# Layers 1 and 2 of a gated graph network: h turned by DMA instead of TensorE, and the adjacency loaded twice

## The chip, the cores and the metric

The kernel runs on one core of a Trainium2 chip. The metric is the device time of one execution in microseconds (us). The engines of the core work side by side, each through its own queue in order: PE (TensorE, matmuls, with PEld for its weight loads), DVE (VectorE), ACT (ScalarE), POOL (GpSimd) and SP (SyncE, which here issues nearly all DMA transfers).

## The reference

There are 64 graphs of N = 256 nodes with D = 256 features each, and a 0/1 adjacency matrix for each. First come three layers of a gated graph network, then a residual and a normalization, then one graph attention layer with another residual and normalization:

```
A = (adj != 0)
h = x
for i in range(3):
    m    = h @ weight[i]
    aggr = A^T @ m                      # per graph: 'bst,bsd->btd'
    h    = gru_cell(aggr, h)            # r, z, n gates of 256 columns each
x = layernorm(x + h)
Wh = x @ W ; s1 = Wh @ a1 ; s2 = Wh @ a2
e  = leaky_relu(s1[:, None] + s2[None, :]) ; e = where(adj > 0, e, -9e15)
out = layernorm(x + softmax(e) @ Wh)
```

The kernel aggregates h before it multiplies by the weight (the weight is folded into the input weights of the gates once, at the start), so each layer needs A^T h and then matmuls with fixed weights.

## The kernel before

**Tiling.** The 64 graphs are taken in 32 pairs (G = 2). The state h of a pair is kept turned, as `hT`: features on the 128 partitions (two halves, d = 0 and 1), the 512 nodes of the two graphs along the free dimension. It is updated in place by each layer. The adjacency of a pair is loaded once by `load_adj` (line 170) into a buffer of the pool `io` that has one copy only (tag "adj"); `ones` (line 318) makes the fp32r matrix A of it, and `masking` (line 327) makes a uint8 mask that is kept, in four buffers, until the pair's attention, some three turns later.

**Split precision.** Matmuls run in fp32r. Operands are cut into an upper part and a rest: `hi` and `lo` for the aggregation, and pieces H, L and D of h and of the aggregate for the gates (`upper`, `lower`, `cross`, lines 128 to 136).

**A layer.** `front(p, i, t, pace)` prepares layer i of pair p. The aggregation wants h with the nodes on the partitions, so `turn` (line 337) transposes `hT` on PE: `from_T` (line 308) issues four 128x128 transposes for each half d into one PSUM bank "pt". ACT casts the bank to `hi` (line 349) and DVE subtracts for `lo` (line 133 through `lower`). For layer 0, x itself already has the nodes on the partitions, and no transpose is needed. `aggregate` (line 375) issues 8 matmuls a half into a bank "pa"; `a_upper` and `a_rest` cut the result. `gates` (line 400) then runs 8 products of 6 or 12 matmuls of 128x512, each into a bank "pga" and a bank "pgb"; ACT evacuates pga, DVE adds pgb, ACT applies sigmoid or tanh, POOL multiplies and blends, and DVE writes the new half of `hT` (line 451).

**PSUM.** There are eight banks of 512 fp32 columns, handed out in rotation by `bank` (line 106) to every user on PE.

**Attention.** `attention(p, t)` (line 490) reads x back, adds h in the turned layout (`vT`), and turns that sum by transfers: `turn` (line 501) issues two DMA transposes, which move 16-bit elements, so that the fp32 words come out as interleaved 16-bit rows in the buffer "wh"; `second` (line 511) gathers low and high halves with four transfers into the buffer "sc"; `join` (line 519) puts them together through `put_together` (line 278), ACT writing the high halves and DVE the low ones. Then follow a normalization, the projection (`project`, L541), scores, the mask (`masked`, L573), softmax, and the combination (L601). The tile in "wh" serves first as the buffer of the transposes and then for the projected features, and the tile in "sc" first for the halves and then for the scores.

**x by transfers.** For pairs from 5 on (`FROM` = 5), x_turned (line 284) and x_joined (line 302) produce `hT` of layer 0 in the same way: a DMA transpose of x into the buffer "x" of `io`, a gather into the buffer "adj" of `io`, and a join on ACT and DVE.

**The order of the work.** It is written out by hand. A clock counts ticks, which advance inside `gates` (12 ticks a block). A step registered with `at(t, step)` or `after(dt, step)` is issued when the clock reaches its tick, and each engine's queue has the instructions in that order. The blocks (pair, layer) are interleaved: a turn of 36 ticks holds layer 0 of pair q, layer 1 of pair q-1 and layer 2 of pair q-2, while the attention of pair q-3 runs beside them. The offsets within a layer's preparation are the tuples `CLOSE`, `LOOSE` and `FIRST` (lines 621 to 623): the first tuple gives the ticks of turn, hi, lo, aggregate, a_upper and a_rest, and the second those of the pieces H, L and D of h.

Of the kernel before, what the change touches and what calls it, by code (L numbers as in the profile page):

```python
# [9 lines left out]
F32 = mybir.dt.float32  # L10
# [9 lines left out]
P = 128  # L20
# [7 lines left out]
def kernel(  # L28
# [230 lines left out]

    pairs = {}  # L260

    def room(kind, shape, p):


        name = f"{kind}_{p}"
        if p < NP - 2:
            return late.tile(shape, F32, tag=kind, name=name, bufs=2 if kind == "v" else 1)
        tag = {"v": "hH", "vT": "hD", "wh": "aH", "sc": "aD"}[kind]
        return work.tile(shape, F32, tag=tag, name=name)
# [5 lines left out]
            nc.tensor.transpose(pt[:, k * P:(k + 1) * P], src[:, k // C, k % C, d * P:(d + 1) * P], ident)  # L275
        after(1, lambda: evacuate(dst[:, d, :], pt))

    def put_together(dst, hi, lo):

        dst = dst.bitcast(U16).rearrange("p (n h) -> p n h", h=2)  # L280
        nc.scalar.copy(dst[:, :, 1], hi)
        nc.vector.tensor_copy(dst[:, :, 0], lo)

    def x_turned(p):

# [38 lines left out]
    def take_x(p):  # L324
        pairs[p].x = loaded.pop(p)

    def masking(p):
        s = pairs[p]
        s.mask = work.tile([P, K, N], U8, tag="mask", name=f"mask_{p}", bufs=4)
        nc.vector.tensor_scalar(s.mask, s.adj.rearrange("p g c n -> p (g c) n"), 0.0, None, op0=ALU.is_le)  # L330

    def front(p, i, t, pace):

        nm = f"{p}_{i}"
        hi, lo, src = [None] * C, [None] * C, [None] * C

        def turn(d):
            s = pairs[p]
            if i == 0:
                if p < FROM:  # L340
                    to_T(s.x, s.hT, d)
            else:
                src[d] = from_T(s.hT, d).rearrange("p (k n) -> p k n", k=K)

        def split(d):
            if i == 0:
                src[d] = nodes(pairs[p].x, d)
            hi[d] = work.tile([P, K, P], F32R, tag=f"hi{d}", name=f"hi{d}_{nm}", bufs=1)
            nc.scalar.copy(hi[d], src[d])
# [24 lines left out]

        def aggregate(d):
            s = pairs[p]
            if d == 0:
                s.ag = pieces(work, [P, C, GN], nm, "a")
            pt = src[d] = bank("pa")
            for g in range(G):  # L380
                todo = [(h[d], c) for c in range(C) for h in (hi, lo)]
                for n, (h, c) in enumerate(todo):
                    nc.tensor.matmul(pt[:, g * N:(g + 1) * N], h[:, g * C + c, :], s.A[:, g, c, :],  # L383
                                     start=(n == 0), stop=(n == len(todo) - 1))

        def a_upper(d):
            upper(pairs[p].ag[0][:, d, :], src[d])

        def a_rest(d):
            H, Lo, Di = [t[:, d, :] for t in pairs[p].ag]  # L390
            lower(nc.vector, Lo, src[d], H)
            cross(Di, src[d], H)

        for d in range(C):
            for dt, step in zip(pace[0], (turn, split, rest, aggregate, a_upper, a_rest)):
                at(t + dt + d, lambda step=step, d=d: step(d))
        for dt, step in zip(pace[1], (h_upper, h_lower, h_cross)):
            at(t + dt, step)
# [91 lines left out]
    def attention(p, t):  # L490
# [10 lines left out]
        def turn(d):  # L501

            if d == 0:
                s.wh = room("wh", [P, G, C, D], p)
                s.first = s.wh.rearrange("p g c d -> p (g c d)").bitcast(U16).rearrange(
                    "p (k b d) -> p k b d", b=2, d=D)
            nc.sync.dma_start_transpose(
                s.first.rearrange("p k b d -> p (k b) d")[:, :, d * P:(d + 1) * P],
                s.vT[:, d, :].bitcast(U16))

        def second():
            s.sc = room("sc", [P, K, N], p)
            s.halves = s.sc.rearrange("p k n -> p (k n)").bitcast(U16).rearrange(
                "p (h k d) -> p h k d", h=2, k=K)
            for h in range(2):
                for b in range(2):
                    nc.sync.dma_start(s.halves[b * 64:b * 64 + 64, h], s.first[h::2, :, b])

        def join(g):
            if g == 0:  # L520
# [13 lines left out]

        def project(k):
            if k == 0:
                s.s1 = work.tile([P, K], F32, tag="s1", name=f"s1_{p}")
                s.s2 = s.sc[:, :, :P]
            pts[k] = bank("pwh")
            for d in range(C):  # L540
                nc.tensor.matmul(pts[k][:, :D + 2], s.vT[:, d, k * P:(k + 1) * P], gw[:, d, :],  # L541
                                 start=(d == 0), stop=(d == C - 1))

        def spread(k):
            rs = s.rs[:, k:k + 1]
            for dst, src in ((s.s1[:, k:k + 1], pts[k][:, D:D + 1]),
                             (s.s2[:, k, :], pts[k][:, D + 1:D + 2].to_broadcast([P, P])),
                             (s.wh[:, k // C, k % C, :], pts[k][:, :D])):
                if k < 2:
                    nc.scalar.activation(dst, src, AF.Copy, scale=rs)  # L550
                else:
                    nc.vector.tensor_scalar(dst, src, rs, None, op0=ALU.mult)
        for k in range(K):
            at(t + 35 + k, lambda k=k: project(k))
            at(t + 36 + k, lambda k=k: spread(k))

        def rows():
            pts[0] = bank("s2")
# [3 lines left out]
        def scores():  # L562
            for k in range(K):
                nc.scalar.activation(s.sc[:, k, :], pts[0][:, (k // C) * N:(k // C + 1) * N], AF.Prelu,
                                     bias=s.s1[:, k:k + 1], alpha=ALPHA)
        at(t + 40, rows)
        at(t + 41, scores)

        s.nm = work.tile([P, K], F32, tag="nm", name=f"nm_{p}")
        s.sm = work.tile([P, K], F32, tag="sm", name=f"sm_{p}")  # L570

        def masked():
            nc.vector.copy_predicated(flat(s.sc), flat(s.mask), neg.to_broadcast([P, K * N]))  # L573
        at(t + 42, masked)
        at(t + 43, lambda: nc.vector.tensor_reduce(s.nm, s.sc, AX.X, ALU.max, negate=True))

        def exps(k):
            nc.scalar.activation(s.sc[:, k, :], s.sc[:, k, :], AF.Exp, bias=s.nm[:, k:k + 1],
# [69 lines left out]
    nc.vector.tensor_add(b_sum, bi, bh)  # L648
    tick()
    ones(0)  # L650
    masking(0)
    load_adj(1)
    tick()
    for parts in PARTS:
# [16 lines left out]
    for n, (p, i) in enumerate(blocks):  # L671
        if n + 1 < len(blocks):
            np_, ni = blocks[n + 1]
            if ni == 0:
                if np_ < FROM:
                    after(1, lambda p=np_: begin(p))
                after(1, lambda p=np_: take_x(p))
                after(2, lambda p=np_: ones(p))
                nxt = np_ + 1
                if nxt < FROM:  # L680
                    after(7, lambda p=nxt: load_x(p))
                elif nxt < NP:
# [12 lines left out]
    while pending:  # L695
        clock[0] = pending[0][0]
        run_due()
# [29 lines left out]
```

## Time and profile before

The three runs took 2168.55 to 2170.91 us, with a median of 2169.64 us; the profiled execution took 2168.29 us, and its span in the trace is 2166.5 us.

| engine | busy, us | share | instructions |
|---|---|---|---|
| PE (matmul) | 2124.7 | 98% | 10508 |
| PEld | 1790.7 | 83% | 10508 |
| DVE | 1735.2 | 80% | 2885 |
| POOL | 1593.0 | 74% | 1114 |
| ACT | 1497.1 | 69% | 2734 |
| DMA queue q1 | | 27.1% of 16 engines | 234816 packets |

A group row of the profile gives line, engine, operation, output and input tile, shape and count, then the total busy time and the mean duration of one in ns, then the idle time of the engine just before these instructions and what ended it. The chain of waits is followed back from the last instruction; its shares tell what set the end. A turn of the steady state lasts 65.1 us (from 999.8 to 1064.95 us in the trace, at the first layer-0 product of two neighbouring turns).

### The profile page before, as it was taken

The numbers are of one execution on the slowest core, as the hardware profiler recorded it, in microseconds if no ns is written. First come the engines' busy times: TensorE is split into PE (matmuls) and PEld (weight loads), VectorE is DVE, ScalarE is ACT, GpSimd is POOL, SyncE is SP. The second block draws the span as 40 slices with busy tenths as digits, with TensorE's granted clock in tenths as the row PEclk, the third lists the DMA queues.
The fourth block names the chain that finished last, engine by engine and source line by source line (L and its number), as shares of the span: only waits on it lengthen the run. The fifth ranks groups of instructions, "written<-read, shape, count | busy, mean of one in ns | idle before, by whom it ended". The sixth has DMA issues, their size and how long they took to land.

```text
span 2166.5 us, 30928 instructions
## 1 busy us (share of the span) xinstructions
PE 2124.7 (98%) x10508; PEld 1790.7 (83%) x10508; DVE 1735.2 (80%) x2885; ACT 1497.1 (69%) x2734; POOL 1593.0 (74%) x1114
## 2 busy tenths in 40 slices
PE   8999999999999999999999999999999999999995
PEld 6788888888888888888888888888888888888873
DVE  5667878888778888778888788888788888788786
ACT  4566677677777677777677777677777677777664
POOL 6688677777777777777777777777777777787671
PEclk9999999999999999999999999999999999999997
DMA  3001322322322222322323323323323223321122
GB/s 117 30 30 49 79 69 69 78 74 64 88 66 71 76 72 67 88 64 74 74 70 72 88 61 76 71 69 76 88 59 78 69 69 78 86 61 49 39 54 64
DMA packets 236765, 150.39 MB, mean 69 GB/s; under 512 B 130304, under 2 KB 228352, under 8 KB 236608
## 3 DMA queue, kind: packets, MB, share of 16 engines
q1 hardware_dynamic: 234816, 146.58, 27.1%
q8 instruction: 84, 1.38, 0.3%
q10 hardware_dynamic: 1616, 1.57, 0.2%
q14 instruction: 73, 0.60, 0.1%
q0 software_dynamic: 176, 0.27, 0.1%
HBM read 52.96 MB, written 33.55 MB: 40 GB/s over the span
## 4 chain that ended last, share of the span: by engine, by line
PE 95%; DVE 2%; POOL 1%; ACT 1%; DMA 0%; issue 0%; POOLq 0%; ACTq 0%; SPq 0%; DVEq 0%
PE pga L412 48%; PE pgb L412 24%; PE pa L383 8%; PE po L601 5%; PE pwh L541 5%; PE pt L311 3%; PE pt L593 1%; PE s L560 1%; DMA rows_hH<-in_L_gnn_w_hh_dram 0%; PE pw L236 0%; POOL t L438 0%; POOL wc2L_wc L147 0%; POOL t L439 0%; DVE v L607 0%; DVE cut L133 0%
## 5 line engine op out<-in xcount | busy, mean ns | idle before, releaser
L438 POOL TENSOR_TENSOR t<-hT,n 128x512 f32<-128x512 f32 x192 | 273.0, 1422 | 392.0 <-ACT n L430 391.8
L412 PE MATMUL pga<-hH,whhH_whh 128*128 128x512 f32 x1152 | 375.7, 407 | 0.0
L412 PE MATMUL pga<-hL,whhL_whh 128*128 128x512 f32 x1152 | 357.6, 392 | 1.0 <-POOL hL L133 1.0
L412 PE MATMUL pgb<-hD,whhD_whh 128*128 128x512 f32 x1152 | 357.5, 391 | 1.0 <-DVE hD L136 1.0
L448 POOL TENSOR_TENSOR n<-n,t 128x512 f32<-128x512 f32 x192 | 274.9, 1432 | 77.8 <-DVE t L421 67.5
L417 ACT ACTIVATE r<-pga 128x512 f32<-128x512 f32 x192 | 114.4, 596 | 289.6 <-PE pga L412 163.4
L439 POOL TENSOR_TENSOR t<-t,z 128x512 f32<-128x512 f32 x192 | 303.4, 1580 | 15.0
L412 PEld LDWEIGHTS pga<-hL,whhL_whh 128*128 128x128 f32 x1152 | 216.3, 188 | 49.2 <-POOL hL L133 1.5
L444 POOL TENSOR_TENSOR n<-n,r 128x512 f32<-128x512 f32 x192 | 256.0, 1333 | 0.9 <-DVE n L421 0.9
L412 PEld LDWEIGHTS pgb<-hD,whhD_whh 128*128 128x128 f32 x1152 | 216.4, 188 | 48.6 <-DVE hD L136 1.4
L133 POOL TENSOR_TENSOR hL<-hT,hH 128x1024 fp32r<-128x1024 f32 x96 | 242.8, 2529 | 11.2 <-ACT hH L130 11.1
L412 PEld LDWEIGHTS pga<-hH,whhH_whh 128*128 128x128 f32 x1152 | 200.4, 189 | 26.6
L419 ACT ACTIVATE n<-pga,bh 128x512 f32<-128x512 f32 x192 | 132.1, 688 | 117.8 <-PE pga L412 112.5
L383 PE MATMUL pa<-A,hi 128*128 128x256 f32 x768 | 202.3, 297 | 0.2 <-DVE A L322 0.2
L421 DVE SCALAR_TENSOR_TENSOR r<-pgb,r 128x512 f32<-128x512 f32 x192 | 131.4, 685 | 82.1 <-ACT r L417 57.1
L383 PE MATMUL pa<-A,lo 128*128 128x256 f32 x768 | 192.2, 283 | 0.0
L136 DVE SCALAR_TENSOR_TENSOR hD<-hH,hT 128x1024 fp32r<-128x1024 f32 x96 | 190.5, 1985 | 0.0
L451 DVE TENSOR_TENSOR hT<-t,n 128x512 f32<-128x512 f32 x192 | 165.6, 863 | 4.3 <-POOL t L439 4.3
L421 DVE SCALAR_TENSOR_TENSOR n<-pgb,n 128x512 f32<-128x512 f32 x192 | 131.2, 683 | 44.4 <-ACT n L419 44.4
L421 DVE SCALAR_TENSOR_TENSOR t<-pgb,t 128x512 f32<-128x512 f32 x192 | 131.2, 683 | 39.4 <-ACT t L417 38.5
L417 ACT ACTIVATE t<-pga 128x512 f32<-128x512 f32 x192 | 114.6, 597 | 68.1 <-PE pga L412 68.1
L430 ACT ACTIVATE r<-r,b_sum 128x512 f32<-128x512 f32 x192 | 139.2, 725 | 23.1 <-DVE r L421 22.6
(138 smaller groups left out, 5365.2 us busy)
## 6 DMA issues: line engine op xcount, KB each, us to landing
x<-in_x_dram SPq DMA_DIRECT2D x32, 512.0 KB, 3.9
adj<-in_adj_dram SPq DMA_DIRECT2D x32, 512.0 KB, 3.9
xT<-hT SPq DMA_DIRECT2D x32, 512.0 KB, 4.1
vT<-xT SPq DMA_DIRECT2D x32, 512.0 KB, 3.6
sc<-wh SPq DMA_DIRECT2D x128, 128.0 KB, 3.4
out_dram<-v SPq DMA_DIRECT2D x32, 512.0 KB, 3.0
second<-first SPq DMA_DIRECT2D x108, 128.0 KB, 3.0
wh<-vT SPq DMA_TRANSPOSE x64, 3.2
```

What stands on the lines that cost most here:

```text
L133: eng.tensor_sub(dst, src, hi.bitcast(F32))
L136: nc.vector.scalar_tensor_tensor(dst, hi.bitcast(F32), 1.0 + U, src, op0=ALU.mult, op1=ALU.subtract)
L383: nc.tensor.matmul(pt[:, g * N:(g + 1) * N], h[:, g * C + c, :], s.A[:, g, c, :], start=(n == 0), stop=(n == len(todo) - 1))
L412: nc.tensor.matmul(pt, w[:, d, o * P:(o + 1) * P], m[:, d, :], start=n in (0, ends + 1), stop=n in (ends, len(todo) - 1))
L417: nc.scalar.activation(dst, a, AF.Copy, scale=1.0 + U)
L421: nc.vector.scalar_tensor_tensor(dst, b, -1.0 / U, dst, op0=ALU.mult, op1=ALU.add)
L430: nc.scalar.activation(dst, dst, func, bias=bias)
L438: nc.gpsimd.tensor_sub(t, h, n)
L439: nc.gpsimd.tensor_mul(t, t, z)
L444: after(2, lambda r=r, n=n: nc.gpsimd.tensor_mul(n, n, r))
L448: after(1, lambda n=n, t=t: nc.gpsimd.tensor_add(n, n, t))
L451: after(lags[2], lambda n=n, t=t, h=h: nc.vector.tensor_add(h, t, n))
```

## The change

For layers 1 and 2 of pairs 5 to 30 (layer 2 up to pair 29), `hT` is turned by transfers instead of on PE. The new `h_turned(p, i, e)` is registered after the gates of layer i: two DMA transposes and a gather of four transfers on SP, and for each half d a join (both 16-bit halves on ACT, into a tile "V" with one buffer), a cast to `hi` on ACT and a subtraction for `lo` on DVE. For the turning after layer 0 it borrows the buffers "wh" and "sc", and after layer 1 the buffers "x" and "adj" of `io`. `front` then skips its first three steps. The other pairs and layers keep the transposes on PE.

To make room, the buffers "wh" and "sc" are released by attention between its two uses of them; its projection comes two ticks later, and so do the scores, the masking and the maximum. The mask is no longer made with A and kept: the adjacency is loaded a second time (`adj_again`), and the mask is made from it just before its use, in one buffer instead of four. The steps of x and of the adjacency are moved by some ticks, and layer 2 from pair 5 on uses `CLOSE` in place of `LOOSE`.

```diff
-    def put_together(dst, hi, lo):
+    def put_together(dst, hi, lo, k=None):
...
-        dst = dst.bitcast(U16).rearrange("p (n h) -> p n h", h=2)
-        nc.scalar.copy(dst[:, :, 1], hi)
-        nc.vector.tensor_copy(dst[:, :, 0], lo)
+        dst = dst.bitcast(U16).rearrange("p (n h) -> p h n", h=2)
+        if k:
+            dst = dst.rearrange("p h (k n) -> p h k n", k=k)
+        nc.scalar.copy(dst[:, 1], hi)
+        if k:
+            nc.scalar.copy(dst[:, 0], lo)
+        else:
+            nc.vector.tensor_copy(dst[:, 0], lo)
...
+    def h_turned(p, i, e):
...
+        s = pairs[p]
+        pool, tags, dt = ((late, ("wh", "sc"), (16, 19, 22)), (io, ("x", "adj"), (12, 22, 25)))[i]
...
+        def first():
+            tmp["a"] = first_of(pool.tile([P, G, C, D], F32, tag=tags[0], name=f"first_h{p}_{i}"))
+            for d in range(C):
+                turn_half(tmp["a"], s.hT, d)
...
+        def second():
+            tmp["b"] = second_of(pool.tile([P, G, C, D], F32, tag=tags[1], name=f"second_h{p}_{i}"))
+            gather(tmp["b"], tmp["a"])
...
+        def join(d):
+            tmp[d] = work.tile([P, K, P], F32, tag="V", name=f"V{d}_{p}_{i}", bufs=1)
+            put_together(tmp[d].rearrange("p k n -> p (k n)"),
+                         *(tmp["b"][:, h, :, d * P:(d + 1) * P] for h in (1, 0)), k=K)
...
+        at(e + dt[0], first)
+        at(e + dt[1], second)
+        for d in range(C):
+            for n, step in enumerate((join, split, rest)):
+                at(e + dt[2] + 3 * d + n, lambda step=step, d=d: step(d))
+        s.by_dma = i + 1
...
-    def masking(p):
-        s = pairs[p]
-        s.mask = work.tile([P, K, N], U8, tag="mask", name=f"mask_{p}", bufs=4)
-        nc.vector.tensor_scalar(s.mask, s.adj.rearrange("p g c n -> p (g c) n"), 0.0, None, op0=ALU.is_le)
...
         for d in range(C):
-            for dt, step in zip(pace[0], (turn, split, rest, aggregate, a_upper, a_rest)):
+            for dt, step in list(zip(pace[0], (turn, split, rest, aggregate, a_upper, a_rest)))[3 * by_dma:]:
                 at(t + dt + d, lambda step=step, d=d: step(d))
...
         for k in range(K):
-            at(t + 35 + k, lambda k=k: project(k))
-            at(t + 36 + k, lambda k=k: spread(k))
+            at(t + 37 + k, lambda k=k: project(k))
+            at(t + 38 + k, lambda k=k: spread(k))
...
-        at(t + 40, rows)
-        at(t + 41, scores)
+        at(t + 42, rows)
+        at(t + 43, scores)
...
+        at(t + 38, adj_again)
+        at(t + 43, mask)
...
-        at(t + 42, masked)
-        at(t + 43, lambda: nc.vector.tensor_reduce(s.nm, s.sc, AX.X, ALU.max, negate=True))
+        at(t + 44, masked)
+        at(t + 45, lambda: nc.vector.tensor_reduce(s.nm, s.sc, AX.X, ALU.max, negate=True))
...
-                after(2, lambda p=np_: ones(p))
+                after(3, lambda p=np_: ones(p))
...
-                    after(22, lambda p=nxt, d=later: d.update(f=x_turned(p)))
-                    after(26, lambda d=later: d["f"]())
-                    after(30, lambda p=nxt: x_joined(p))
-                    after(31, lambda p=nxt: load_x(p))
-                early = 3 if np_ + 1 < FROM else 0
-                after(19 - early, lambda p=np_: masking(p))
-                after(20 - early if nxt < FROM else 32, lambda p=nxt: load_adj(p))
-            front(np_, ni, clock[0], CLOSE if n and np_ == blocks[n - 1][0] else LOOSE if ni else FIRST)
+                    after(25, lambda p=nxt, d=later: d.update(f=x_turned(p)))
+                    after(29, lambda d=later: d["f"]())
+                    after(32, lambda p=nxt: x_joined(p))
+                    after(32, lambda p=nxt: load_x(p))
+                after(5 if nxt < FROM else 34, lambda p=nxt: load_adj(p))
+            front(np_, ni, clock[0], 
+                  CLOSE if n and np_ == blocks[n - 1][0] or ni == 2 and np_ >= FROM else LOOSE if ni else FIRST)
...
         if i == L - 1:
             attention(p, clock[0])
+        elif FROM <= p and p + i + 1 < NP:
+            h_turned(p, i, clock[0])
```

More of the change, by code (lines that the diff above doesn't have):

```diff
@@ L260, with room @@
     pairs = {}
-    def room(kind, shape, p):
-        name = f"{kind}_{p}"
+    def room(kind, shape, p, name=None):
+        name = f"{name or kind}_{p}"
         if p < NP - 2:
@@ new lines, in first_of, with second_of, turn_half, gather @@
+    def first_of(t):
+        return t.rearrange("p g c d -> p (g c d)").bitcast(U16).rearrange("p (k b d) -> p k b d", b=2, d=D)
+    def second_of(t):
+        return t.rearrange("p g c d -> p (g c d)").bitcast(U16).rearrange("p (h k d) -> p h k d", h=2, k=K)
+    def turn_half(dst, src, d):
+        nc.sync.dma_start_transpose(dst.rearrange("p k b d -> p (k b) d")[:, :, d * P:(d + 1) * P],
+                                    src[:, d, :].bitcast(U16))
+    def gather(dst, src):
+        for h in range(2):
+            for b in range(2):
+                nc.sync.dma_start(dst[b * 64:b * 64 + 64, h], src[h::2, :, b])
@@ new lines, in h_turned, with split, rest @@
+    def h_turned(p, i, e):
+        s = pairs[p]
+        pool, tags, dt = ((late, ("wh", "sc"), (16, 19, 22)), (io, ("x", "adj"), (12, 22, 25)))[i]
+        tmp = {}
+        def first():
[9 more added lines that the diff above has]
+                         *(tmp["b"][:, h, :, d * P:(d + 1) * P] for h in (1, 0)), k=K)
+        def split(d):
+            s.hi[d] = work.tile([P, K, P], F32R, tag=f"hi{d}", name=f"hi{d}_{p}_{i + 1}", bufs=1)
+            nc.scalar.copy(s.hi[d], tmp[d])
+        def rest(d):
+            s.lo[d] = work.tile([P, K, P], F32R, tag=f"lo{d}", name=f"lo{d}_{p}_{i + 1}", bufs=1)
+            lower(nc.vector, s.lo[d], tmp[d], s.hi[d])
+        s.hi, s.lo = [None] * C, [None] * C
+        at(e + dt[0], first)
[4 more added lines that the diff above has]
+        s.by_dma = i + 1
@@ L325, in take_x @@
         pairs[p].x = loaded.pop(p)
-    def masking(p):
-        s = pairs[p]
-        s.mask = work.tile([P, K, N], U8, tag="mask", name=f"mask_{p}", bufs=4)
-        nc.vector.tensor_scalar(s.mask, s.adj.rearrange("p g c n -> p (g c) n"), 0.0, None, op0=ALU.is_le)
     def front(p, i, t, pace):
         nm = f"{p}_{i}"
+        by_dma = getattr(pairs.get(p), "by_dma", None) == i
         hi, lo, src = [None] * C, [None] * C, [None] * C
+        if by_dma:
+            hi, lo = pairs[p].hi, pairs[p].lo
         def turn(d):
@@ L503, in turn @@
             if d == 0:
[L504 to L509, printed above, removed]
-        def second():
[L512 to L517, printed above, removed]
+                s.first = first_of(room("wh", [P, G, C, D], p, "first"))
+            turn_half(s.first, s.vT, d)
+        def second():
+            s.halves = second_of(room("sc", [P, G, C, D], p, "second"))
+            gather(s.halves, s.first)
         def join(g):
@@ L536, in project @@
             if k == 0:
+                s.wh = room("wh", [P, G, C, D], p)
+                s.sc = room("sc", [P, K, N], p)
                 s.s1 = work.tile([P, K], F32, tag="s1", name=f"s1_{p}")
@@ L565, in scores, with adj_again, mask @@
                                      bias=s.s1[:, k:k + 1], alpha=ALPHA)
-        at(t + 40, rows)
-        at(t + 41, scores)
+        at(t + 42, rows)
+        at(t + 43, scores)
         s.nm = work.tile([P, K], F32, tag="nm", name=f"nm_{p}")
         s.sm = work.tile([P, K], F32, tag="sm", name=f"sm_{p}")
+        def adj_again():
+            load_adj(p)
+        def mask():
+            s.mask = work.tile([P, K, N], U8, tag="mask", name=f"mask_{p}", bufs=1)
+            nc.vector.tensor_scalar(s.mask, loaded_adj.pop(p).rearrange("p g c n -> p (g c) n"), 0.0, None,
+                                    op0=ALU.is_le)
+        at(t + 38, adj_again)
+        at(t + 43, mask)
         def masked():
             nc.vector.copy_predicated(flat(s.sc), flat(s.mask), neg.to_broadcast([P, K * N]))
-        at(t + 42, masked)
-        at(t + 43, lambda: nc.vector.tensor_reduce(s.nm, s.sc, AX.X, ALU.max, negate=True))
+        at(t + 44, masked)
+        at(t + 45, lambda: nc.vector.tensor_reduce(s.nm, s.sc, AX.X, ALU.max, negate=True))
         def exps(k):
@@ L650 @@
     ones(0)
-    masking(0)
     load_adj(1)
```

## The prediction

> **What bounds the kernel now.** I read the page's busy table first, then the chain that ended last, then the groups for the lines that the diff touches, then one turn of the steady state (1000 to 1065 us) engine by engine, and last the waits of SP's queue.
>
> ```profile
> PE 2124.7 (98%) x10508; PEld 1790.7 (83%) x10508; DVE 1735.2 (80%) x2885; ACT 1497.1 (69%) x2734; POOL 1593.0 (74%) x1114
> ...
> PE pga L412 48%; PE pgb L412 24%; PE pa L383 8%; PE po L601 5%; PE pwh L541 5%; PE pt L311 3%; PE pt L593 1%; PE s L560 1%; DMA rows_hH<-in_L_gnn_w_hh_dram 0%; PE pw L236 0%; POOL t L438 0%; POOL wc2L_wc L147 0%; POOL t L439 0%; DVE v L607 0%; DVE cut L133 0%
> ```
>
> ```profile
> 1000.00:1065.00 65.00, 65.00 (x326) 55.06 (x324) 53.70 (x90) 46.50 (x86) 49.33 (x35) 1.00 0.29 73
> ```
>
> In that window (columns: PE, PEld, DVE, ACT, POOL busy, clock, DMA share, GB/s) PE has no idle time in 65.00 us, while DVE has 11.3, ACT 18.5 and POOL 15.7. The chain is 95% PE, and the transposes that the change takes off PE (L311) are on it with 3%. So a PE instruction removed shortens the span, and one added elsewhere costs nothing until PE waits for it.
>
> ```profile
> L311 PE MATMUL pt<-ident,hT 128*128 128x128 f32 x512 | 77.1, 273 | 0.0
> L349 ACT CAST hi<-pt 128x512 fp32r<-128x512 f32 x128 | 74.6, 583 | 7.1 <-PE pt L311 7.1
> L133 DVE TENSOR_TENSOR lo<-pt,hi 128x512 fp32r<-128x512 f32 x128 | 87.6, 686 | 11.3 <-ACT hi L349 11.2
> L281 ACT COPY hT<-second 128x512 uint16<-128x512 uint16 x54 | 37.6, 768 | 0.0
> L451 DVE TENSOR_TENSOR hT<-t,n 128x512 f32<-128x512 f32 x192 | 165.6, 863 | 4.3 <-POOL t L439 4.3
> ```
>
> ```profile
> 1003.64 1.03 PE L541 MATMUL pwh<-gw,vT 128*128 128x258 f32 x4
> 1004.51 0.60 PE L311 MATMUL pt<-ident,hT 128*128 128x128 f32 x4
> 1004.86 0.72 PE L412 MATMUL pga<-hH,whhH_whh 128*128 128x512 f32 x2
> 1005.42 0.40 PE L412 MATMUL pga<-hL,whhL_whh 128*128 128x512 f32 x1
> ```
>
> The last fence is the timeline of PE (start, length). From the start of four transposes to the start of hL is 0.91 us, and two 128x512 matmuls alone take 2 x 0.227; so a group of four costs 0.455 us. Over the 69 groups of the trace that stand between L412 matmuls the median is the same 0.4545 us.
>
> ```profile
> SPq L616 <- ACT v L478: 563.0, 32, 19.6
> SPq L173 <- DVE hT L282: 331.5, 27, 12.5
> SPq L299 <- DVE mask L330: 128.9, 27, 5.5
> SPq L517 <- DMA wh<-vT: 60.4, 34, 3.1
> ```
>
> These are waits of SP's queue. It issues in order, and stands for long stretches behind a store or an adjacency load; nothing on PE waits for it now.
>
> **What the Trainium skill says.** "TensorE: Matmul & The Clock Gate", Part 4: PE-mode transpose, gives about 275 ns for one in a kernel; the trace has 273 ns as a duration, but only 0.455/4 = 0.114 us of PE's time, which is what counts. "DMA: Bandwidth & Descriptors", DMA Transpose (X-bar), allows 2-byte types only, which is why an fp32 tile goes as 16-bit halves and must be rejoined; the uint16 copies of L281 are that price. Its Rules for kernel authors say that a DMA reading what an earlier DMA wrote must wait for its completion: the 60.4 us of L517 above. "SBUF — State Buffer", Who interferes with whom: a DVE instruction with two SBUF inputs contends with a GpSimd one that reads SBUF; the trace agrees (L451 863 ns against 686 for the PSUM form of L133), and says that ACT waits for nobody.
>
> **The change part by part.** A turn is three blocks, 36 ticks, 65.1 us. Layer-1 turning through DMA is made for pairs 5 to 30, layer-2 for 5 to 29: 51 times.
>
> Removed from PE: 51 x 2 groups of four = 408 of 512 transposes, 102 x 0.455 = 46.4 us. Bounds: the busy column, 77.1/512 x 408 = 61.4 us, is the high end (it shares out overlap); I take the start-to-start value. Two PSUM banks less per turned layer are also taken.
>
> Added to ACT: 204 copies (hi and lo of each half-tile, both on ACT) x 0.768 = 156.7 us; 102 casts read SBUF instead of PSUM, 609 against 583 ns (the row of hi<-x), 2.7 us. That is 6.2 us a turn on 18.5 idle; ACT goes to about 1656 us, 78% of the new span. It matters only as lateness: where copies stand ahead of the evacuations of pga, banks come free later. In the trace I matched each bank's last reader with the matmul that takes the bank eight allocations later: typically 3 to 6 us lie between, with 1.2 and 0.3 us at 1028.3 and 1030.2. The 0.3 us is a bank of the removed transposes. Layer 2's joins come just there (ticks 13 to 17, about 1023 to 1031), behind the exponentials, where ACT has no gap from 1020.0 to 1029.2. PE comes there 0.9 to 1.8 us sooner, ACT is about 1 us later, and after re-counting the banks without the transposes' two, 1.5 us are left at the tightest place. Layer 1's joins (ticks 34 to 38, about 1061 to 1068) make ACT at most 2 us later against 4 to 5 us of margin; the spread of the attention moved two ticks back makes room. I count 0 to 1 us of PE wait a turn, taken as 2 us in all.
>
> DVE: 102 subtractions now have two SBUF inputs, 0.68 to 0.86 us, so 0 to 18 us, and POOL may lose as much as 102 x 0.68 = 69 us (its twins run 1.29 us alone and up to 2.16 beside such an instruction), 2.7 us a turn on 15.7 idle. The 32 masks stay 32, now made beside the scores. Hidden behind PE both.
>
> SP and DMA: added are 102 half transposes, 204 gathers, 32 adjacency loads. Issue: 1.32 us a transpose, 2.6 for four gathers, 0.4 a load: 10.9 us a turn. Occupancy from the packet records of the window: 1.26 us of all engines a half transpose, 2.9 four gathers, 1.8 a load, so 4 x 1.26 + 2 x 2.9 + 1.8 = 12.7 us on 19; the share goes from 0.29 to about 0.50. The adjacency buffer (one) gets four tenants a turn: the adjacency, its reload, layer 2's second half, the x second half. Past SP's queue I followed one turn in before's times. Mask done about 1014, gather 1016, landed 1019; join wants it at 1023: 4 us spare. The x transpose then lands at 1024; its gather waits for the second join on ACT, 1030, is issued until 1032.4 and landed about 1035; behind it stand load x, the attention's transposes (which wait for L601 until 1035.6 anyway) and load adj. x_joined wants it at about 1036. Attention's gather lands about 1047.5; layer 1's transposes follow, then the stash, then its gather 1053.5 to 1056, landed 1058 to 1059; ACT wants it at 1058.7. This is the tightest: 0 to 1 us of wait on ACT, inside the bank margin.
>
> The moves: projection and spread +2 ticks, scores to maximum +2 with the exponentials unmoved, x turning +3, ones +1, layer 2's aggregation +1 with hL and hD earlier: all order only, with PE's work unchanged. At the end, one group of four pwh matmuls goes behind the last gate product, and the mask for pair 31 loads only after a store waiting for ACT (2137.8 before) and a landing of 3.9 us, so about 2142.5 against its use at 2143.5: 0 to 2 us, taken as 1.
>
> Sum against the profiled span of 2166.5: -46.4 + 2 + 1 = -43.4, so 2123.1; the median of the runs is 3.1 above that span, which gives 2169.6 - 43.4 = 2126.
>
> **The rivals.** (A) The forecast: hidden, 2117 to 2136.
> (B) Half is given back: ACT late by the joins at both places, PE waiting about 0.9 us a turn for banks, 26 x 0.9 = 23, so 2149 (2136 to 2162). For: ACT has no gap at the table loads. Against: the large gaps (3.4 us at 1035.6) right after, and fewer banks taken.
> (C) No change: transposes filled time that PE would wait anyway, 2165 to 2174. Against: PE's idle before L311 is 0.0, and bank margins are positive.
> (D) Slower: layer 1's gather lands too late. ACT then stands at the first join with r, z and t evacuations behind it, and PE runs out of banks. It decides when the landing is more than 4 us (bank margin) + 1.8 us (what a turn saves, 4 groups of 0.455) after 1058.7, that is after about 1064.5, 6 us later than I put it; doubled DMA occupancy might stretch seven chained transfers by nearly 1 us each. At 7 us late PE loses 3 us a turn and saves 1.8, so 26 x 1.2 = 31 us more than before: 2201. Against: transfers land in 3 to 4 us now, and the SP order leaves waiting time of its own.
>
> **How the numbers follow.** A 0.72, B 0.14, C 0.04, D 0.10. Forecast 2126. A, B to 2157 hold a little over 0.8, so the range is 2116 to 2157; A alone is 2117 to 2136. Before's three runs spread over 0.1%; 0.2% (4.3 us) is what can be told from no change: faster 0.86, same 0.04, slower 0.10.
>
> **What would show it.** Right: PE still 97% or more with 10100 matmuls, turns of about 63.3 us, ACT near 1655, DMA near 45%, waits of PE for banks not seen. B: PE idle before pga or pgb matmuls released by ACT L417's successors. D: ACT copies V<-second waiting on DMA by several us. Wrong if PE's steady state shows gaps of over a microsecond, or the end after the last gate product is much longer than 61 us.

## The result, and the profile after

The changed kernel takes 2134.62 us (median of four runs, 2133.43 to 2135.79) against 2170.18 for the kernel before (median of four runs): ratio 0.9837, with a 95% interval of 0.982 to 0.9854. That is 35.6 us less; the forecast was 2126, and 2134.6 lies inside its range of 2116 to 2157. The profiled span is 2133.2 us against 2166.5, so 33.3 us less where the sum gave 43.4. Eight to ten microseconds are missing (8.6 by the medians, 10.1 by the profiled spans), and the experiments are about them.

The busy table and the chain by line, after:

```profile
PE 2087.5 (98%) x10100; PEld 1748.8 (82%) x10100; DVE 1788.7 (84%) x2885; ACT 1609.8 (75%) x2938; POOL 1605.2 (75%) x1114
...
PE 94%; DVE 2%; POOL 1%; ACT 1%; issue 1%; DMA 0%; POOLq 0%; ACTq 0%; SPq 0%; DVEq 0%
PE pga L466 48%; PE pgb L466 24%; PE pa L437 8%; PE po L659 5%; PE pwh L589 5%; PE pt L651 1%; PE s L608 1%; PE pt L367 1%; DMA rows_hH<-in_L_gnn_w_hh_dram 0%; PE pw L236 0%; POOL n L502 0%; DVE sc L631 0%; DVE cut L133 0%; POOL t L492 0%; DVE nm L633 0%
```

The 408 matmul instructions are gone (10508 to 10100), and the transposes of h have fallen from 3% of the chain to 1% (L367). The same 65 us window of the steady state (PE, PEld, DVE, ACT, POOL busy, clock, DMA share, GB/s), and the groups for the lines that carry the new work:

```profile
1000.00:1065.00 65.00, 65.00 (x318) 54.70 (x317) 57.43 (x92) 51.81 (x96) 51.37 (x37) 1.00 0.50 118
```

```profile
L133 DVE TENSOR_TENSOR lo<-V,hi 128x512 fp32r<-128x512 f32 x102 | 100.5, 986 | 15.5 <-ACT hi L327 15.5
L283 ACT COPY V<-second_h 128x512 uint16<-128x512 uint16 x102 | 78.9, 773 | 11.8 <-DVE lo L133 11.8
L285 ACT COPY V<-second_h 128x512 uint16<-128x512 uint16 x102 | 78.7, 771 | 0.0
L327 ACT CAST hi<-V 128x512 fp32r<-128x512 f32 x102 | 63.1, 618 | 0.0
```

PE still has no idle time in the window, and the joins (L283) wait for no transfer: the only releaser in their row is `lo` on DVE, which still reads the one buffer V. So the mechanism is as forecast, and the loss is in pieces too small for a busy column. I therefore cut every run at three places of the PE timeline: the first product of pair 7's layer 0, that of pair 31's layer 0, and the start of the last gate product; the tail goes on to the end of the last issue on SP, that of the last store. All in us:

| kernel | up to pair 7 | 24 turns, 7 to 31 | last turn | tail |
|---|---|---|---|---|
| before | 413.6 | 1563.2 | 128.4 | 57.7 |
| after | 413.5 | 1523.4 | 130.1 | 62.8 |
| b_no_turns | 415.3 | 1519.5 | 126.6 | 59.0 |
| a_no_h | 413.6 | 1566.4 | 129.2 | 64.1 |
| a_tail_ticks | 413.4 | 1523.4 | 131.0 | 58.8 |
| a_pace | 411.3 | 1523.1 | 127.4 | 63.0 |
| a_both | 411.1 | 1523.5 | 128.2 | 58.9 |
| a_late | 411.2 | 1523.2 | 129.0 | 64.1 |
| a_reduce | 412.3 | 1577.2 | 133.0 | 63.7 |
| a_all | 412.5 | 1577.2 | 132.7 | 59.9 |
| a_hd | 413.1 | 1557.6 | 130.7 | 62.8 |
| a_all2 | 410.7 | 1554.2 | 128.9 | 58.8 |
| a_joins_twice | 412.3 | 1636.1 | 133.0 | 62.9 |
| a_gather3 | 418.1 | 1661.4 | 136.0 | 62.3 |

The first column scatters by 2 us between kernels whose beginnings hardly differ (the turn of pair 0 alone takes 30.8 to 32.6 us), the last two by about 1 us (after against a_late). The 24 turns agree within 0.4 us over five kernels, and are what small effects are read from.

### The profile page after: what moved, and what is told of

It is laid out like the page before. It is cut to its first block, busy times and chain, and to the rows that moved or that the text cites. A ratio compares the mean times of both kernels' runs of the same rounds, so it can differ in the third digit from the quotient of the medians.

```text
span 2133.2 us, 30903 instructions
## 1 busy us (share of the span) xinstructions
PE 2087.5 (98%) x10100; PEld 1748.8 (82%) x10100; DVE 1788.7 (84%) x2885; ACT 1609.8 (75%) x2938; POOL 1605.2 (75%) x1114
## 3 DMA queue, kind: packets, MB, share of 16 engines
q1 hardware_dynamic: 414912, 216.86, 43.5%
## 4 chain that ended last, share of the span: by engine, by line
PE 94%; DVE 2%; POOL 1%; ACT 1%; issue 1%; DMA 0%; POOLq 0%; ACTq 0%; SPq 0%; DVEq 0%
PE pga L466 48%; PE pgb L466 24%; PE pa L437 8%; PE po L659 5%; PE pwh L589 5%; PE pt L651 1%; PE s L608 1%; PE pt L367 1%; DMA rows_hH<-in_L_gnn_w_hh_dram 0%; PE pw L236 0%; POOL n L502 0%; DVE sc L631 0%; DVE cut L133 0%; POOL t L492 0%; DVE nm L633 0%
## 5 line engine op out<-in xcount | busy, mean ns | idle before, releaser
L492 POOL TENSOR_TENSOR t<-hT,n 128x512 f32<-128x512 f32 x192 | 253.1, 1318 | 391.1 <-ACT n L484 391.0
L493 POOL TENSOR_TENSOR t<-t,z 128x512 f32<-128x512 f32 x192 | 291.3, 1517 | 15.1
L502 POOL TENSOR_TENSOR n<-n,t 128x512 f32<-128x512 f32 x192 | 281.0, 1464 | 21.4 <-DVE t L475 11.1
L498 POOL TENSOR_TENSOR n<-n,r 128x512 f32<-128x512 f32 x192 | 288.4, 1502 | 4.5 <-DVE n L475 4.5
L475 DVE SCALAR_TENSOR_TENSOR r<-pgb,r 128x512 f32<-128x512 f32 x192 | 131.3, 684 | 166.4 <-ACT r L471 139.9
L133 POOL TENSOR_TENSOR hL<-hT,hH 128x1024 fp32r<-128x1024 f32 x96 | 255.7, 2664 | 13.3 <-ACT hH L130 13.2
L466 PEld LDWEIGHTS pga<-hH,whhH_whh 128*128 128x128 f32 x1152 | 206.3, 189 | 31.9
L136 DVE SCALAR_TENSOR_TENSOR hD<-hH,hT 128x1024 fp32r<-128x1024 f32 x96 | 186.4, 1942 | 0.0
L505 DVE TENSOR_TENSOR hT<-t,n 128x512 f32<-128x512 f32 x192 | 171.3, 893 | 5.6 <-POOL t L493 5.6
L473 ACT ACTIVATE n<-pga,bh 128x512 f32<-128x512 f32 x192 | 133.5, 696 | 50.7 <-PE pga L466 46.4
L471 ACT ACTIVATE t<-pga 128x512 f32<-128x512 f32 x192 | 115.3, 601 | 57.3 <-DVE hT L505 38.2
L475 DVE SCALAR_TENSOR_TENSOR t<-pgb,t 128x512 f32<-128x512 f32 x192 | 131.0, 682 | 25.6 <-ACT t L471 22.5
L437 PEld LDWEIGHTS pa<-A,lo 128*128 128x128 f32 x768 | 146.3, 191 | 6.2 <-issue 0.2
```

What stands on the lines that cost most here:

```text
L133: eng.tensor_sub(dst, src, hi.bitcast(F32))
L136: nc.vector.scalar_tensor_tensor(dst, hi.bitcast(F32), 1.0 + U, src, op0=ALU.mult, op1=ALU.subtract)
L466: nc.tensor.matmul(pt, w[:, d, o * P:(o + 1) * P], m[:, d, :], start=n in (0, ends + 1), stop=n in (ends, len(todo) - 1))
L471: nc.scalar.activation(dst, a, AF.Copy, scale=1.0 + U)
L475: nc.vector.scalar_tensor_tensor(dst, b, -1.0 / U, dst, op0=ALU.mult, op1=ALU.add)
L492: nc.gpsimd.tensor_sub(t, h, n)
```

## Experiment 1: the transposes left out

```diff
+            elif FROM <= p and p + i < NP:
+                src[d] = s.hT[:, d, :].rearrange("p (k n) -> p k n", k=K)
             else:
                 src[d] = from_T(s.hT, d).rearrange("p (k n) -> p k n", k=K)
```

> The kernel before, with the 408 transposes of h left out where the changed kernel turns h by transfers, and nothing put in their place: the split and its rest read hT as it lies, so what is aggregated in these layers is not the reference's. It measures the price of the transposes on TensorE by itself, without copies, transfers, waits or moved ticks. The sum of the prediction (0.455 us start to start for each of 102 groups) expects 46.4 us off, about 2124; the busy column would give 61.4 us off, about 2109. A rival from the trace after, where a turn is 1.66 us shorter for its four groups (0.41 us a group): 42 us off, about 2128, which would mean that the price was taken a tenth too high and that little was given back in the steady turns.

Measured: 2125.16 us against 2169.83, ratio 0.979 (0.9776 to 0.9804), 44.7 us less. The 24 turns fall by 1563.2 - 1519.5 = 43.7 us, and 24 x 4 x 0.455 is 43.68. The start-to-start price of a group is exact here, the busy column's 61.4 us is excluded, and so is the reading of 0.41 us a group from the turns of after: the price was right, and something was given back.

## Experiment 2: everything but the turning of h

```diff
-        elif FROM <= p and p + i + 1 < NP:
-            h_turned(p, i, clock[0])
...
-                  CLOSE if n and np_ == blocks[n - 1][0] or ni == 2 and np_ >= FROM else LOOSE if ni else FIRST)
+                  CLOSE if n and np_ == blocks[n - 1][0] else LOOSE if ni else FIRST)
```

> The changed kernel with h turned on TensorE again in all layers (no turning transfers, gathers or joins of h, and the old lead of layer 2's split), keeping its other parts: the attention's projection, scores and masking two ticks later, the mask made late from a second load of adjacency, the x of the next pair turned later. If the missing 10 us comes from these parts (theory: about 5 us in the tail, up to 1 at the start), it is slower than the kernel before by 4 to 6 us, 2174 to 2176, with a tail after the last gate product of about 63 us against 57.7. If the loss is all from the transfers and copies of h, it takes the time of before, 2170, within 1 us.

Measured: 2179.53 us against 2169.83, ratio 1.0041 (1.0029 to 1.0054): 9.7 us slower, twice what I expected. So about as much as is missing lies in the parts that only make room; against this kernel, after is 2179.53 - 2134.62 = 44.9 us faster, as much as leaving the transposes out is worth. In the table, of the profiled executions, it is 10.4: 3.2 us in the 24 turns, 0.8 in the last turn, which is within the scatter, and 6.4 in the tail.

The 3.2 us I had not expected. They show in one row, the weight loads of the products that read hD, of after, a_no_h, and b_no_turns in this order:

```profile
L466 PEld LDWEIGHTS pgb<-hD,whhD_whh 128*128 128x128 f32 x1152 | 214.0, 188 | 55.2 <-issue 8.4
```

```profile
L466 PEld LDWEIGHTS pgb<-hD,whhD_whh 128*128 128x128 f32 x1152 | 214.1, 188 | 55.6 <-issue 8.4 <-DVE hD L136 1.7
```

```profile
L414 PEld LDWEIGHTS pgb<-hD,whhD_whh 128*128 128x128 f32 x1152 | 216.2, 188 | 49.0 <-DVE hD L136 1.7
```

Idle time of 8.4 us put down to "issue" (the profile shows no wait that ended it) is there in both kernels with the moved attention and not in the third. The timeline of after shows one of them (start, length, engine; in brackets the idle time before and what ended it):

```profile
1001.92 0.69 DVE L475 SCALAR_TENSOR_TENSOR r<-pgb,r 128x512 f32<-128x512 f32 x1 [0.25 <-PE pgb L466]
1002.52 1.21 DVE L633 TENSOR_REDUCE nm<-sc 128x4 f32<-128x1024 f32 x1
...
1005.44 1.15 DVE L505 TENSOR_TENSOR hT<-t,n 128x512 f32<-128x512 f32 x1
...
1006.51 2.31 DVE L136 SCALAR_TENSOR_TENSOR hD<-hH,hT 128x1024 fp32r<-128x1024 f32 x1
...
1008.93 0.30 PEld L466 LDWEIGHTS pgb<-hD,whhD_whh 128*128 128x128 f32 x2 [0.29 <-issue]
1008.96 0.70 PE L466 MATMUL pgb<-hD,whhD_whh 128*128 128x512 f32 x2
```

hD ends at 1008.82, and the first product of layer 1 that reads it starts 0.14 us later, with a gap of 0.29 us at the weight load. Two matmul spacings there are 0.29 and 0.31 us instead of 0.227, so 0.15 us a turn. Over pairs 8 to 27 the product starts 1.41 us (median) after the end of hD in the kernel before, 1.30 in b_no_turns, and 0.15 in a_no_h and after. The maximum (L633) stood ahead of hD in DVE's order before too, but also ahead of `r` (L421 then, L475 now), which waits for a product of PE; two ticks later, it stands behind `r`, and hD starts 1.33 us later (median, from the start of layer 1's first product); 0.47 of this is the addition to hT (L505), which takes 1.15 us there instead of 0.68. Nothing else makes the turns longer: from before to a_no_h a turn grows by 0.13 us (median of 22), the two spacings at hD by 0.15, and the shifts of the other gate products add up to nothing.

## Experiments 3 and 4: the tail and the last turn

a_tail_ticks puts the last three pairs' attentions back to the old ticks:

```diff
+        q = 2 if p >= NP - 3 else 0
...
-            at(t + 37 + k, lambda k=k: project(k))
+            at(t + 37 - q + k, lambda k=k: project(k))
```

and in the same way spread, rows, scores, the second adjacency load, mask, masking and maximum.

> The changed kernel, with projection, spread, rows, scores, mask and masking of the last three pairs' attentions (29 to 31) two ticks earlier, where the kernel before has them; all other pairs as changed. Theory: the tail grew because pair 31's projection and rows now stand behind pair 30's weight transposes and output products on TensorE; 4 to 5 us come back, about 2130, and the tail is 58 to 59 us instead of 62.8. Rival: the tail grew because the late mask is made in line on VectorE, which this leaves in place: at most 1 us comes back.

Measured: 2131.25 us, ratio 0.9815 (0.9801 to 0.983); the tail is 58.8 us against 62.8. The medians of after, this kernel and the next lie so close that their intervals overlap; the table's last two columns decide. The PE timeline of after and then of this kernel, where the two differ:

```profile
2101.40 1.40 PE L651 MATMUL pt<-ident,sc 128*128 128x128 f32 x4 [4.72 <-ACT sc L636]
2102.59 1.93 PE L589 MATMUL pwh<-gw,vT 128*128 128x258 f32 x4
...
2106.79 1.89 PE L659 MATMUL po<-wh,sc 128*128 128x256 f32 x8
2108.52 0.60 PE L608 MATMUL s<-ident,sc 128*128 128x128 f32 x4
```

```profile
2094.54 3.66 PE L590 MATMUL pwh<-gw,vT 128*128 128x258 f32 x16
2099.77 0.33 PE L652 MATMUL pt<-ident,sc 128*128 128x128 f32 x1 [1.57 <-ACT sc L637]
...
2104.29 0.90 PE L609 MATMUL s<-ident,sc 128*128 128x128 f32 x3 [0.30 <-ACT sc L599]
2105.50 5.93 PE L660 MATMUL po<-wh,sc 128*128 128x256 f32 x16 [0.31 <-DVE sc L670]
```

In after, the second half of pair 31's projection stands in PE's order behind pair 30's weight transposes, which wait 4.72 us for the exponentials, and its score rows (`s`) stand behind an output product of pair 30. With the old ticks the projection fills that wait. The edit moves the late mask two ticks as well, so the run alone does not clear it; the trace of after does: pair 31's mask is done at 2110.19, and the scores that it masks at 2110.78.

a_pace changes one pair. Its layer 2 gets back the old offsets as a whole: h's transposes three ticks earlier, hi two, lo, the aggregation, its upper part and hH one, and hL two and hD three later.

```diff
-                  CLOSE if n and np_ == blocks[n - 1][0] or ni == 2 and np_ >= FROM else LOOSE if ni else FIRST)
+                  CLOSE if n and np_ == blocks[n - 1][0] or ni == 2 and FROM <= np_ < NP - 2 else LOOSE if ni else FIRST)
```

> The changed kernel, with the pace of before for layer 2 of pair 30 alone, which still turns h on TensorE: its hL and hD are cut one and three ticks later. Theory: in the last turn TensorE waits for VectorE (1.6 us near 2035) because hD went ahead of the masking and of the evacuations in a stretch where VectorE is the last; 2 to 3 us come back, about 2132. Rival: VectorE's load there (the mask and the joins' rests) is what is late, in whatever order: less than 0.5 us changes.

Measured: 2131.24 us, ratio 0.9822 (0.9807 to 0.9836); the last turn is 127.4 us against 130.1 (129.0 in a_late below, which differs from after only by the tick of one gather). In after DVE made mask, hD and masking in this order (in a_pace the mask takes 0.68 us, and hD stands behind the masking), and PE then stood twice:

```profile
2016.44 2.75 DVE L625 TENSOR_SCALAR mask<-adj 128x1024 uint8<-128x1024 int32 x1
2019.11 2.31 DVE L136 SCALAR_TENSOR_TENSOR hD<-hH,hT 128x1024 fp32r<-128x1024 f32 x1
2021.34 1.38 DVE L631 COPY_PREDICATED_SCALAR sc<-mask,neg 128x1024 f32 x1
```

```profile
2034.58 0.73 PE L466 MATMUL pgb<-aD,wc2D_wc 128*128 128x512 f32 x2 [0.41 <-ACT n L473]
2036.18 1.99 PE L659 MATMUL po<-wh,sc 128*128 128x256 f32 x8 [0.86 <-DVE sc L669]
```

In a_pace neither wait is there. Pair 30's layer 2 still turns h on PE in after; the change moved its steps all the same. That hD is the step that counts is argued from this order; the run moves the others with it.

## Experiment 5: both

> The changed kernel with the attentions of pairs 29 to 31 at their old ticks and the old pace of hL and hD for layer 2 of pair 30; all steady turns as changed. Each alone gave 3.4 us back. If the tail and the last turn are separate losses, both come back: 2127 to 2129, with a tail of 58.5 to 59.5 us and 127 to 128 us from the start of pair 31 to the last gate product. If they share a cause, 2130 to 2131.

Measured: 2128.94 us (2127.02 to 2129.54), ratio 0.981 (0.9796 to 0.9823). Tail 58.9, last turn 128.2: the two losses are separate, and 5.7 us come back by the medians, 5.8 in the last two columns of the table. By its median it is the fastest run that computes the reference.

## Experiments 6 and 7: trying to win back hD's 0.15 us

a_reduce puts the maximum behind hD on DVE, with the exponentials a tick later; a_all adds the edits of experiment 5.

```diff
-        at(t + 45, lambda: nc.vector.tensor_reduce(s.nm, s.sc, AX.X, ALU.max, negate=True))
+        at(t + 47, lambda: nc.vector.tensor_reduce(s.nm, s.sc, AX.X, ALU.max, negate=True))
...
-            at(t + 47 + k // 2, lambda k=k: exps(k))
+            at(t + 48 + k // 2, lambda k=k: exps(k))
```

> The changed kernel with the row maximum of the scores (L633) two ticks later and the exponentials one tick later, so that on VectorE the maximum stands behind the cut hD of the next block instead of ahead of it. Theory: in every steady turn TensorE's first product of layer 1 waits 0.15 us for hD (its weights are loaded 0.29 us late), because the masking and the maximum now stand ahead of it on VectorE; with the maximum behind, the 24 turns from pair 7 to pair 31 take 1519.5 us instead of 1523.4, the same as with the transposes simply left out, so 3 to 4 us come back (about 2131), less what one tick later costs in the tail (0 to 2). Rival: the 0.15 us comes from the matmuls' other neighbours on TensorE, and the turns stay at 1523.

> Three edits to the changed kernel together: the attentions of pairs 29 to 31 at their old ticks, the old pace of hL and hD for layer 2 of pair 30, and for the other pairs the maximum behind hD. If the three losses are separate, 3.5 (steady turns) + 2.7 (last turn) + 4 (tail) come back: about 2125, the time of the kernel before without the transposes. If they share a cause, for instance VectorE's load in the last turn, only 5 to 7 us come back: 2128 to 2130.

Measured: 2192.11 us (ratio 1.0099, 1.0084 to 1.0114) and 2189.16 us (1.0086, 1.0071 to 1.0101). Both slower than before, with 1577.2 us for the 24 turns. A miss; yet the part that I meant to cure is cured: hD now ends 1.67 us ahead of its product, and both spacings are back at 0.227. So hD's lateness is what made them longer. a_hd is a milder way, which moves only hT's last addition behind hD; a_all2 adds the edits of experiment 5.

```diff
-            after(lags[2], lambda n=n, t=t, h=h: nc.vector.tensor_add(h, t, n))
+            after(lags[2] + (i == L - 1), lambda n=n, t=t, h=h: nc.vector.tensor_add(h, t, n))
```

> The changed kernel with only the last addition to hT of layer 2 (L505) one tick later, so that on VectorE it stands behind the cut hD of the next layer 1 instead of ahead of it; nothing on ScalarE moves. Theory: hD comes 1.2 us earlier, TensorE's 0.15 us wait in each steady turn goes, the 24 turns from pair 7 to pair 31 take 1519.5 to 1520 us instead of 1523.4: 3 to 4 us back, about 2131. Rival: the 0.15 us is not hD's: no change, 2134.

> The edit of a_hd together with the old ticks for the attentions of pairs 29 to 31 and the old pace for layer 2 of pair 30. If the three losses are separate, 3.5 + 2.7 + 3 to 4 us come back: 2124 to 2126, as the kernel before without the transposes. If the tail and the last turn share a cause, 2127 to 2129.

Measured: 2166.99 us (0.9986, 0.9978 to 0.9994) and 2157.31 us (0.9943, 0.993 to 0.9957). Again the "issue" idle is gone, and again the turns are longer. (hD does not start earlier in a_hd; it ends earlier, since it takes 1.2 us instead of 2.3; see the last section.) PE's waits in a_hd, and one row of all waits (who waited for whom: us in total, times, longest):

```profile
PE po L659 <- DVE sc L669: 27.0, 26, 1.2
```

```profile
ACT t L471 <- DVE hT L505: 87.6, 78, 1.6
```

ACT's evacuation into `t` waits for the later addition (87.6 us, where after has 38.2), the exponentials behind it are late, and the output product `po` then waits once a turn. In after the same stretch reads (ACT, DVE and PE of one turn):

```profile
1012.76 0.58 ACT L471 ACTIVATE r<-pga 128x512 f32<-128x512 f32 x1
...
1013.37 0.69 DVE L475 SCALAR_TENSOR_TENSOR r<-pgb,r 128x512 f32<-128x512 f32 x1 [2.22 <-ACT r L471]
...
1015.46 0.66 DVE L669 COPY sc<-pt 128x512 f32<-128x512 f32 x1
...
1016.36 1.89 PE L659 MATMUL po<-wh,sc 128*128 128x256 f32 x8
```

DVE stands 2.22 us for ACT, which is behind exponentials, two join copies, a table load and a sigmoid; everything behind on DVE slides along, and the copy `sc` that `po` reads ends 0.24 us before `po` starts. From the end of that copy to the start of the first `po` is 2.92 us in the kernel before, 3.10 in a_no_h, 2.02 in b_no_turns, 0.27 in after (medians of 24 turns), and 0.15 with PE standing in a_reduce and a_hd. The turning of h took up all but about 0.1 us of it. Counted from the start of layer 1's first product (medians), the two join copies make the evacuation `r` 1.33 us later on ACT, `lo` adds 0.6 ahead of the copy `sc` on DVE, and PE comes to `po` 0.9 us sooner without its transposes. Whatever makes ACT later at that place goes straight to PE: `r` starts 1.73 us later in a_hd than in after and 2.28 in a_reduce, where the exponentials wait 32.5 us in all for the maximum, and the median turn is 1.70 and 2.24 us longer. Over the 24 turns that is 34.2 and 53.8 us.

## Experiments 8 to 10: how near were rivals B and D?

For B, every join copy of h is made twice:

```diff
+            nc.scalar.copy(dst[:, 1], hi)
+            nc.scalar.copy(dst[:, 0], lo)
             nc.scalar.copy(dst[:, 0], lo)
```

> The changed kernel with every uint16 copy of h's joins made twice on ScalarE (204 more copies of 0.77 us, eight a turn, 6.2 us a turn). It asks how near rival B was, ScalarE late and TensorE without banks. Theory: ScalarE's idle time and the bank margins of 2 to 6 us take most of it: 0 to 0.4 us a turn, 2135 to 2145. Rival B, if single joins had already used up the margin: 0.9 us or more a turn, above 2158.

Measured: 2250.86 us (1.0372, 1.0355 to 1.039). Of 6.2 us more ACT work a turn, 4.7 us become PE time, at three places:

```profile
PE pwh L591 <- ACT r L473: 35.7, 26, 1.5
PE po L661 <- DVE sc L671: 30.9, 26, 1.2
...
PE pa L439 <- DVE A L380: 10.8, 25, 0.5
```

My expectation was wrong by 100 us. An engine busy 75% of the time had almost nothing left where it counted.

For D I first gave layer 1's gather a later tick:

```diff
-        pool, tags, dt = ((late, ("wh", "sc"), (16, 19, 22)), (io, ("x", "adj"), (12, 22, 25)))[i]
+        pool, tags, dt = ((late, ("wh", "sc"), (16, 22, 22)), (io, ("x", "adj"), (12, 22, 25)))[i]
```

> The changed kernel with the gather of layer 1's h issued three ticks later, in the tick of its first join, so that it lands about 4 us after ScalarE wants it (1.2 us before, now). It tests rival D's mechanism and its threshold (4 us of bank margin). Theory: ScalarE stands about 4 us a turn at the first join, and TensorE, whose banks are evacuated behind it with 2 to 4 us to spare, loses 0 to 2 us a turn: 2135 to 2185. If ScalarE's wait cost nothing at all, the margin was wider than the bank count says; if it costs the full 4 us a turn (2240), there was none.

Measured: 2132.8 us (0.9827, 0.9812 to 0.9841), the time of after. It shows nothing on D: the gather was issued as soon after the transposes as in after (2.5 us behind the end of the stash of hT in both, medians of 26 turns), because a later tick changes its place in SP's order only, and nothing of SP stood in between. So the gather was made three times:

```diff
-            gather(tmp["b"], tmp["a"])
+            for _ in range(1 if i else 3):
+                gather(tmp["b"], tmp["a"])
```

> The changed kernel with the gather of layer 1's h made three times over (8 more transfers of 128 KB a turn, to the same place). They issue for 2.6 us a set, so the last lands about 5.2 us later: 4 us after ScalarE wants it for the first join. Rival D's mechanism: ScalarE stands there about 4 us a turn; by D's own threshold (4 us of bank margin) TensorE loses 0 to 0.5 us a turn, 2134 to 2147; by the tightest banks of the trace behind that place (1.9 and 2.2 us) about 2 us a turn, near 2185. If ScalarE does not stand at all, the doubled traffic costs nothing either, about 2133.

Measured: 2283.84 us (1.0525, 1.0511 to 1.054). The waits, and PE around one of them with the window behind:

```profile
ACT V L283 <- DMA second_h<-first_h: 172.2, 26, 7.2
...
PEld pga L467 <- ACT z L472: 103.6, 26, 4.6
```

```profile
1045.43 1.03 PE L590 MATMUL pwh<-gw,vT 128*128 128x258 f32 x4
1050.14 1.22 PE L467 MATMUL pga<-hH,whhH_whh 128*128 128x512 f32 x2 [3.68 <-ACT z L472]
```

```profile
1050.00:1052.60 2.60, 2.46 (x6) 1.98 (x7) 1.89 (x3) 2.60 (x6) 2.52 (x2) 0.50 0.01 3
```

Rival D's chain is there as it was described: ACT stands 172.2/26 = 6.6 us a turn at the join, and PE runs out of banks. PE loses 5.75 us a turn (138 us in the 24): 3.95 between a projection and the next product, most of the rest because the next matmuls run at a granted clock of 0.50. So ACT's wait at this place costs PE nothing up to about 6.6 - 3.95 = 2.7 us (an estimate from these two waits), not 4. In after the same gather, issued by 1042.0, has landed at 1045.2, 1.5 us before the join at 1046.7 (1.2 in the median of 26 turns), and D never starts.

## Why the prediction was right, and where it was off

- **Removed, 46.4 us.** Right. Experiment 1 gives 44.7 by the medians and the exact 1.82 us a turn; the busy column would have been wrong by 15 us.
- **PE's bank waits, +2.** Small, as forecast: for the turning itself, with layer 2's new pace, the 24 turns are 43.0 us shorter in after than in a_no_h, of 43.7, so 0.7 us are given back. The place was wrong. "1.5 us are left at the tightest place" counted PSUM banks only. The tightest place was a data wait, `po` for DVE's copy `sc`, at 0.27 us, and I had not followed DVE's order behind ACT there. Forecast A came true by a narrow margin.
- **The moves, "order only", 0, and the end, +1.** This is the step that failed: experiment 2 prices it at 9.7 us. By the table it is 3.2 in the turns (hD), 0.8 in the last turn and 6.4 in the tail. I priced the end by what goes behind the last gate product and by the mask's landing; I did not ask what two ticks do to the order of pair 31's projection against pair 30's transposes. A further step of the change, `CLOSE` for layer 2, cost 2.7 and 2.8 us in the last turn (after against a_pace, a_tail_ticks against a_both; 1.6 by a_late against a_pace).
- **Sum.** -44.9 (h turned by transfers, after against a_no_h) + 9.7 = -35.2, against -35.6 measured. The two steps share a_no_h, so that they add up is no check; it says that the turning gave all it promised and the moves took a fifth of it.
- **ACT, 1656.** Measured 1609.8: the copies took 0.772 us each as forecast, but neighbouring instructions overlap in the trace, so the busy time grew by 112.7 instead of 159. **DVE, +0 to 18.** Measured +53.5; the subtraction from SBUF takes 0.986 us, not 0.86 (102 x 0.30 = 30.6 us over the old 0.686); DVE's low halves of the joins of x and of the attention, which the sum left out, took 43 us more, and other groups less. In experiment 1, where hT is the subtraction's other input, it took 1.251. **POOL**, up to 69: 12.2. **DMA** 43.5% and turns of 63.47 us, near the forecast 45% and 63.3.
- **Rival B** was refuted for the change as it is, and is the nearest danger: joins at twice the length are slower than before. **C** falls with experiment 1. **D** has the right mechanism, and did not occur: the gather lands 1.2 us before the join, where I had put it 0 to 1 us late; the threshold was set about 1.3 us too high.

## What to carry to other kernels

Price an instruction on the bound engine by the start-to-start time it takes up there; and price every instruction that is merely moved by what it now stands ahead of on its own engine, at the end of the program as well as in the steady state. Before adding work to a side engine, look for the smallest distance between the end of what it produces, directly or through a third engine's order, and the start of its use: its mean busy share does not show it.

## What the runs showed of the hardware

- After 3.68 us without matmuls PE came back at a granted clock of 0.50, and the 128x512 matmuls ran 0.43 us apart instead of 0.227 for over 2 us. The Trainium skill, "TensorE: Matmul & The Clock Gate", Part 1, gives an idle window of about 3.4 us for this. a_gather3 is near it: PE's 24 gaps at this place last 3.13 to 4.24 us by the trace, whose matmul ends are modelled, and after each of them the next eight gate matmuls take 1.3 to 2.4 us longer than in after.
- The same hD (L136, 128x1024, two SBUF inputs) took 2.31 us in after, where a multiplication on POOL (L493, 1.62 us) had begun 0.39 us before it, and 1.23 us in a_hd, where both began at the same time and POOL's took 2.37. "SBUF — State Buffer", Who interferes with whom, says that the order of issue decides who is held. The first case fits that; in the second the two starts lie within 0.01 us, and the trace does not tell which was issued first.
